# Gates multiplied in place in six broadcast buffers, and two kinds of store issued by ScalarE instead of SyncE

## The chip, the cores and the metric

The kernel runs on one core of a Trainium2 chip. The metric is the device time of one execution in microseconds (us), the median of several runs; lower is better. The profile is of one separate execution, in which every engine's instructions and the DMAs are recorded. Engines are named as in the profile: PE is TensorE, PEld its weight loads, DVE is VectorE, ACT is ScalarE, POOL is GpSimd, SP is SyncE. A "q" after the name (SPq) means the engine's sequencer, which issues DMAs and waits.

## The reference

Two layers on 32 images of 128 channels by 56 x 56 (3,136 tokens of 128 values each). What matters here is the second half of layer 1, a mixture of eight experts of which each token uses two:

```python
# layer 0
x = x + conv3x3(sign(groupnorm(x)), sign(w)) * Alpha
# layer 1
t = tokens(x)                                   # (32, 3136, 128)
n = layernorm(t)
t = t + (n @ Wq + bq) * sum_over_tokens((n @ Wk + bk) * (n @ Wv + bv))
n = layernorm(t)
p = softmax(n @ router_w + router_b)            # 8 experts
top_p, top_i = top_k(p, 2); top_p /= top_p.sum()
expert_out = einsum('bnd,edc->bnec', n, expert_w) + expert_b
t = t + einsum('bnk,bnkc->bnc', top_p, take(expert_out, top_i))
```

## The kernel before, in words

**Two ways to compute the experts.** A chunk is 128 tokens; an image has 25, the last of 64; a block is four chunks (512 tokens). The first blocks of each image (`DENSE`: 8 chunks of images 0 to 15, 12 of images 16 to 27, all 25 of images 28 to 31) are computed densely, with all eight experts and a gate that is zero for six of them. The other chunks are sorted by their pair of experts: their rows are scattered to DRAM (L1365), loaded again as tiles of one pair (L1662), multiplied by two experts (L1687), stored (L1730), gathered back by image (L1444), transposed (L1459), copied to a buffer `o` (L1467) and stored to the output (L1471).

**The dense path.** After routing, `gate_turn` transposes the gates into PSUM, `gate_out` (ACT, L1028 and L1033) copies them to `gt_sb` and, split in bf16 parts, to `gt_parts`. `gate_store` (SP, L1038) writes `gt_sb` to a DRAM tile `gp`, two of which alternate; `parts_store` (SP, L1061) writes the parts to `gb`. For block b and pair of experts k, a unit n, `spread` (SP, L1132) reads two rows of `gp` back, broadcast to all 128 partitions, into `bc`: 128 x 2 x 512 floats, 512 KB. With k = 0 it also loads the parts into `gt` (L1129, three DMAs). `gated` (DVE, L1141) multiplies the block's transposed tokens `tt` by both gate rows into a buffer `gated`; `experts` (PE, L1159) multiplies that by two expert matrices and accumulates over the eight experts in the PSUM bank `ff`; `finish` (DVE, L1170) adds the bank to `tt`, and `store` (SP, L1175) writes it out.

**Buffers.** `bc` has four buffers and `gated` two; `o` has two. A `bc` is free for the next `spread` when its `gated` step is done. A `gated` buffer is free when its matmuls are done.

**What sets the order.** No loop order is written. Each step is entered by `at` with a due time, an engine, a cost, the steps it comes after, the rings that it takes a buffer of and those that it frees. `in_order` (L116) plays the engines against these costs and fixes one order per engine for the whole kernel. Changing a ring's size, an engine or a cost can therefore move any instruction. On the chip each engine keeps its order and waits on semaphores. SP issues the loads of x (L315), the broadcasts, the tile loads, the pads (L1584) and all stores, in one queue. ACT issues DMAs only in the first 17 us (weights and the second and third image). The DMAs that SP and ACT issue share eight completion semaphores, taken in turn in the program's order, and a DMA waits until the one eight places before it has landed.

Of the kernel before, what the change touches and what calls it, by code (L numbers as in the profile page):

```python
# [44 lines left out]
F32 = mybir.dt.float32  # L45
# [4 lines left out]
ALU = mybir.AluOpType  # L50
# [4 lines left out]
C = 128  # L55
# [3 lines left out]
N_EXP = 8  # L59
# [6 lines left out]
WIDE = PER * C  # L66
# [29 lines left out]
LAG = 0.12  # L96
BANKS, EMPTIES = ("ps", "acc", "ff"), 7.0
ROOM = dict(
    ps=5, acc=1, ff=2, y=3, qs=3, tt=4, bc=4, gt=2, gated=2,
    t_in=3, turned=2, v=3, w=2, back=12, sent=4, o=2,  # L100
)

# [83 lines left out]
def conv_attn_moe_kernel(  # L186
# [19 lines left out]
    nc = tc.nc  # L206
    n_img, _, height, width = x.shape
# [29 lines left out]
    bpool = ctx.enter_context(tc.tile_pool(name="bpool", bufs=3))  # L237
    dpool = ctx.enter_context(tc.tile_pool(name="dpool", bufs=2, space=DRAM))
    ps = ctx.enter_context(tc.tile_pool(name="ps", bufs=5, space=PSUM))
# [45 lines left out]
    rb_bc = const.tile([C, N_EXP], F32, name="rb_bc")  # L285
    n_g = 9 * N_EXP
    eb9 = spool.tile([n_g, C], F32, tag="bq_kv", name="eb9")
    eb_row = bpool.tile([1, N_EXP * C], F32, tag="gated", bufs=2, name="eb_row")
    w_bin = const.tile([C, TAPS, C], BF16, name="w_bin")
    xs = const.tile([C, height + 2, width + 2], BF16, name="xs")  # L290
    nc.gpsimd.memset(xs, 0.0)
# [252 lines left out]
    def plan_image(i: int):  # L544
        s = base(i)
        d = {"x": x_all[i % HELD], "tok": tok_all[i % HELD]}
# [3 lines left out]
        n_sort = n_ck - n_dense  # L550
# [142 lines left out]
        for b in range(n_conv):  # L693
# [4 lines left out]
                take=["ps"],  # L698
# [5 lines left out]
        for g in range(n_blk):  # L704
            b = min(n_conv - 1, (cols_of(g)[1] - 1) // (ROWS * width))
            due = s + 4 + 5.5 * b
# [4 lines left out]
                take=["ps"],  # L711
# [105 lines left out]
        for g in range(n_blk):  # L817
# [8 lines left out]
                take=[] if g else ["acc"], free=[("y", ("scaled", i, g))],  # L826
# [208 lines left out]

        def gate_store():
            gp = dpool.tile([n_gb, N_EXP, WIDE], F32, tag="gp", name=f"gp_{i}")
            nc.sync.dma_start(  # L1038
                gp.rearrange("(h b) e (c t) -> (b e c) h t", h=max(1, n_half // 2), c=PER),
                d["gt_sb"],  # L1040
            )
            d["gp"] = gp
# [11 lines left out]
        def parts_store():  # L1054
# [37 lines left out]
            + [("gate_store", i - 1)],  # L1092
        )
        at(
            s + 138, ("gate_store", i), "SP", 0.45, gate_store,
            after=[("gate_out", i), ("spread", i - 2, last_units(i - 2))], delay=GATE_LANDS,
        )
        at(
# [24 lines left out]
        def spread(b, k):  # L1123
            n = cols_of(b)[1] - cols_of(b)[0]
            if k == 0:
                gt = bpool.tile([n_g, WIDE], BF16, tag="gt", bufs=2, name=f"gt_{i}_{b}")
                rows = d["gb"][b, :, :, :n].rearrange("j e t -> (j e) t")
                for r in range(0, n_g, n_g // 3):
                    nc.sync.dma_start(gt[r : r + n_g // 3, :n], rows)  # L1129
                d["gt", b] = gt  # L1130
            bc = bpool.tile([C, 2, WIDE], F32, tag="bc", bufs=4, name=f"bc_{i}_{b}_{k}")
            nc.sync.dma_start(  # L1132
                bc[:, :, :n],
                d["gp"][b, 2 * k : 2 * k + 2, :n].unsqueeze(0).to_broadcast([C, 2, n]),
            )
            d["bc", b, k] = bc

        def gated(b, k):
            n = cols_of(b)[1] - cols_of(b)[0]
            g = bpool.tile([C, 2, WIDE], F32, tag="gated", bufs=2, name=f"gated_{i}_{b}_{k}")  # L1140
            nc.vector.tensor_tensor(  # L1141
                g[:, :, :n],
                d["tt", b][:, :n].unsqueeze(1).to_broadcast([C, 2, n]),
                d.pop(("bc", b, k))[:, :, :n],
                ALU.mult,
            )
            d["gated", b, k] = g

        def experts(b, k):
            n = cols_of(b)[1] - cols_of(b)[0]  # L1150
            if k == 0:
                d["ff", b] = ps_ff.tile([C, WIDE], F32, tag="ff", name=f"ff_{i}_{b}")
                nc.tensor.matmul(  # L1153
                    d["ff", b][:, :n], lhsT=eb_w, rhs=d.pop(("gt", b))[:, :n], start=True, stop=False
                )
            g = d.pop(("gated", b, k))
            for j in range(2):
                e = 2 * k + j
                nc.tensor.matmul(  # L1159
                    d["ff", b][:, :n],  # L1160
                    lhsT=ew_d[:, e * C : (e + 1) * C],
                    rhs=g[:, j, :n],
                    start=False,
                    stop=(e == N_EXP - 1),
                )
# [15 lines left out]
        for b in dense_blocks:  # L1181
            share = (cols_of(b)[1] - cols_of(b)[0]) / WIDE
            n = b * pairs
            at(
                begin + n * unit - 4, ("tt_turn", i, b), "PE", 0.45 * share, to_channels, b,
                after=[("project_add", i, c // Q_GROUP) for c in blocks[b]]
                + [("gated", i, n - 2), ("gate_turn", i)]
                + [("tt_turn", i, b - 1) if b else ("tt_turn", i - 1, last_dense(i - 1))],
                take=["ps", "tt"],
            )  # L1190
            at(
                begin + n * unit - 3, ("tt_out", i, b), "ACT", 0.47 * share, to_channels_out, b,
                after=[("tt_turn", i, b)], free=[("ps", ("tt_turn", i, b))],
            )
            for k in range(pairs):
                n = b * pairs + k
                at(
                    begin + n * unit - 12, ("spread", i, n), "SP", 0.43 + 1.3 * (k == 0), spread, b, k,
                    after=[("gate_store", i), ("spread", i, n - 1), ("spread", i - 1, last_unit)]
                    + ([("parts_store", i)] if k == 0 else []),  # L1200
                    take=["bc"] if k else ["bc", "gt"], delay=SPREAD_LANDS,
                )
                at(
                    begin + n * unit, ("gated", i, n), "DVE", 1.14 * share, gated, b, k,
                    after=[("spread", i, n), ("tt_out", i, b)]
                    + [("gated", i, n - 1) if n else ("gated", i - 1, last_unit)],
                    take=["gated"], free=[("bc", ("spread", i, n))], slack=0.5,
                )
                at(
                    begin + n * unit + 2, ("experts", i, n), "PE",  # L1210
                    (1.74 + 0.22 * (k == 0)) * share, experts, b, k,
                    after=[("gated", i, n), ("experts", i, n - 1)],
                    take=[] if k else ["ff"],
                    free=[("gated", ("gated", i, n))] + ([] if k else [("gt", ("spread", i, n))]),
                )
            at(
                begin + n * unit + 4, ("finish", i, b), "DVE", 0.60 * share, finish, b,
                after=[("experts", i, n)],
                free=[("ff", ("experts", i, b * pairs))],
            )  # L1220
            at(
                begin + n * unit + 5, ("store", i, b), "SP", 0.43, store, b,
                after=[("finish", i, b)], free=[("tt", ("tt_turn", i, b))], delay=STORE_LANDS,
            )
# [243 lines left out]

        def back_store(b):
            lo, hi = cols_of(b)  # L1470
            nc.sync.dma_start(  # L1471
                out[i].rearrange("c h w -> c (h w)")[:, lo:hi], d.pop(("o", b))[:, : hi - lo]
            )

# [8 lines left out]
        for b in range(n_dense // PER, n_blk):  # L1483
            share = len(blocks[b]) / PER
            for c in blocks[b]:
                at(
                    due + each * k / n_sort, ("gather", i, c), "POOL", 1.5, gather, c,
                    after=[("result_rows", i)]
                    + [("gather", i, c - 1) if k else ("gather", i - 1, n_ck - 1)]
                    + [("tile_store", group, q) for q in range(quads_of(group))],  # L1490
                    take=["back"], delay=GATHER_LANDS,
                )
                k += 1
            at(
                due + each * k / n_sort + 5, ("back_turn", i, b), "PE", 0.45 * share, back_turn, b,
                after=[("gather", i, c) for c in blocks[b]], take=["ps"],
                free=[("back", ("gather", i, c)) for c in blocks[b]],
            )
            at(
                due + each * k / n_sort + 6, ("back_out", i, b), "ACT", 0.47 * share, back_out, b,  # L1500
                after=[("back_turn", i, b)], take=["o"], free=[("ps", ("back_turn", i, b))],
            )
            at(
                due + each * k / n_sort + 8, ("back_store", i, b), "SP", 0.43, back_store, b,
                after=[("back_out", i, b)], free=[("o", ("back_out", i, b))], delay=STORE_LANDS,
            )

# [370 lines left out]
```

## Time and profile before

| | |
|---|---|
| Median of 3 runs | 2172.5 us (2171.1 to 2178.69) |
| The profiled execution | 2270.18 us, of which the span from first to last instruction is 2268.4 us |
| Mean granted TensorE clock in it | 0.975 |
| Busy, of the span | PE 2103.4, DVE 1970.1, ACT 1531.2, POOL 1041.1 us |
| `gated`, L1141 | 384 times, 450.7 us in all |
| `experts`, L1159 | 1536 matmul records, 711.5 us in all |
| DMA engines | 54.7% of their time for queue q1, 8.2% for q0, 0.8% for q10 |
| Moved | 448.58 MB, mean 198 GB/s |

The profiled execution is longer than the median of the runs, so sums from the profile are held against its own span. In a row of a group, the figures are the busy time in all, the mean of one in ns, the engine's idle time just before these instructions, and what ended most of it. In the rows of slices, the span is cut into 40 parts of 56.7 us and each digit is the busy share in tenths. In a row of waits, the engine and line that waited come first, then what ended the wait, then total us, times, and the longest. In a timeline, the columns are start, duration, engine, line, operation, and in brackets the idle time before it. A wait for several semaphores is put down to the one that came last.

### The profile page before, as it was taken

The numbers are of one execution on the slowest core, as the hardware profiler recorded it, in microseconds if no ns is written. First come the engines' busy times: TensorE is split into PE (matmuls) and PEld (weight loads), VectorE is DVE, ScalarE is ACT, GpSimd is POOL, SyncE is SP. The second block draws the span as 40 slices with busy tenths as digits, with TensorE's granted clock in tenths as the row PEclk, the third lists the DMA queues.
The fourth block names the chain that finished last, engine by engine and source line by source line (L and its number), as shares of the span: only waits on it lengthen the run. The fifth ranks groups of instructions, "written<-read, shape, count | busy, mean of one in ns | idle before, by whom it ended". The sixth has DMA issues, their size and how long they took to land.

```text
span 2268.4 us, 45320 instructions
## 1 busy us (share of the span) xinstructions
PE 2103.4 (93%) x12074; PEld 1449.1 (64%) x12074; DVE 1970.1 (87%) x6074; ACT 1531.2 (68%) x4917; POOL 1041.1 (46%) x1013
## 2 busy tenths in 40 slices
PE   5899999899999999789999999988999999999888
PEld 2666656557777776457676776655676666676544
DVE  4899999999989999688888889988898798789865
ACT  5667776668888887468777867655877776574311
POOL 3044443333433325466443644676654446233563
PEclk9989999999999999899999999999999999999999
DMA  4155544465665565377667766667767777878788
GB/s 166 30 175 177 167 153 141 138 184 184 203 186 165 176 181 168 110 219 252 194 202 220 226 198 202 215 214 240 225 195 232 217 203 247 249 214 270 222 278 273
DMA packets 324364, 448.58 MB, mean 198 GB/s; under 512 B 61832, under 2 KB 222128, under 8 KB 324112
## 3 DMA queue, kind: packets, MB, share of 16 engines
q1 hardware_dynamic: 294384, 382.80, 54.7%
q0 software_dynamic: 28144, 56.14, 8.2%
q10 hardware_dynamic: 1584, 6.75, 0.8%
q8 instruction: 102, 1.67, 0.3%
q14 instruction: 150, 1.23, 0.2%
HBM read 319.51 MB, written 126.00 MB: 196 GB/s over the span
## 4 chain that ended last, share of the span: by engine, by line
PE 42%; DVE 5%; DMA 3%; issue 2%; ACT 2%; another core or an unknown queue 1%; SPq 0%; POOL 0%; DVEq 0%; ACTq 0%; POOLq 0%
PE ff L1159 14%; PE to L1687 7%; PE cv L642 6%; PE q L863 3%; PE gram L744 3%; PE turn L1669 2%; PE back_ps L1459 2%; PE xt L667 2%; DVE gated L1141 1%; DMA back<-res,res_no 1%; PE l L1114 1%; DMA out_dram<-o 1%; PE ff L1153 1%; DMA bc<-gp 0%
## 5 line engine op out<-in xcount | busy, mean ns | idle before, releaser
L1365 POOL DMA_INDIRECT rows<-tok,row_no x428 | 524.3, 1225 | 570.5 <-ACT tok L1358 235.8
L1159 PE MATMUL ff<-gated,ew_d 128*128 128x512 f32 (+1 forms) x1536 | 711.5, 592 | 23.8 <-DVE gated L1141 19.8
L1444 POOL DMA_INDIRECT back<-res,res_no x428 | 485.4, 1134 | 464.1 <-PE back_ps L1459 264.1
L1141 DVE TENSOR_TENSOR gated<-tt,bc 128x1024 f32<-128x1024 f32 x384 | 450.7, 1180 | 92.2 <-PE ff L1159 29.9
L642 PE MATMUL cv<-xs,w_bin 128*128 128x440 bf16 (+3 forms) x2016 | 429.8, 362 | 18.5 <-ACT xs L599 10.0
L1159 PEld LDWEIGHTS ff<-gated,ew_d 128*128 128x128 f32 x1536 | 274.5, 193 | 258.6 <-issue 202.2
L1705 ACT ACTIVATE v<-to,t_in 128x128 f32<-128x128 f32 x528 | 255.3, 484 | 138.1 <-PE to L1687 74.6
L642 PEld LDWEIGHTS <-w_bin 128*128 128x128 bf16 x2016 | 200.1, 100 | 187.8 <-issue 38.3
L1687 PEld LDWEIGHTS to<-ew_s,turned 128*128 128x128 f32 x2112 | 260.8, 194 | 57.8 <-issue 32.4
L877 ACT ACTIVATE qs<-q,r 128x136 f32<-128x136 f32 (+1 forms) x800 | 247.6, 406 | 70.3 <-PE q L863 35.1
L1687 PE MATMUL to<-ew_s,turned 128*128 x2112 | 273.3, 279 | 18.2 <-ACT turned L1675 8.1
L735 ACT ACTIVATE y<-tok,r 128x128 f32<-128x128 f32 (+1 forms) x800 | 257.0, 428 | 24.3 <-PE gram L744 10.4
L863 PE MATMUL q<-move,x 128*128 128x144 f32 (+1 forms) x1600 | 239.9, 295 | 12.7 <-issue 3.7
L863 PEld LDWEIGHTS q<-move,x 128*128 128x128 f32 (+1 forms) x1600 | 213.6, 193 | 42.4 <-issue 21.1
L744 PEld LDWEIGHTS gram<-y 128*128 128x128 f32 (+1 forms) x1600 | 203.3, 192 | 53.9 <-issue 40.4
L744 PE MATMUL gram<-y 128*128 128x129 f32 (+1 forms) x1600 | 217.8, 281 | 12.9 <-issue 8.1
L682 DVE BATCH_NORM_STATS2 st<-tok 128x6 f32<-128x128 f32 (+1 forms) x800 | 185.4, 279 | 31.9 <-ACT tok L673 26.9
L1712 ACT ACTIVATE w<-to,t_in 128x128 f32<-128x128 f32 x528 | 208.6, 395 | 0.0
L893 DVE BATCH_NORM_STATS2 st<-tok 128x6 f32<-128x128 f32 (+1 forms) x800 | 198.1, 284 | 6.3
L673 ACT COPY tok<-xt 128x512 f32<-128x512 f32 (+1 forms) x224 | 121.2, 561 | 99.9 <-PE xt L667 71.6
L653 DVE SCALAR_TENSOR_TENSOR x<-cv,alpha_col,x 128x448 f32<-128x448 f32 x224 | 151.3, 676 | 40.1 <-PE cv L642 7.2
L890 DVE TENSOR_TENSOR tok<-tok,qs 128x408 f32<-128x408 f32 (+1 forms) x288 | 156.1, 542 | 29.4 <-ACT tok L882 24.1
(229 smaller groups left out, 2896.0 us busy)
## 6 DMA issues: line engine op xcount, KB each, us to landing
bc<-gp SPq DMA_DIRECT2D x368, 512.0 KB
x<-in_x_dram SPq DMA_DIRECT2D x116, 392.0 KB
t_in<-rows SPq DMA_DIRECT2D x528, 66.0 KB
res<-v SPq DMA_DIRECT2D x132, 256.0 KB
out_dram<-o SPq DMA_DIRECT2D x100, 256.0 KB
out_dram<-tt SPq DMA_DIRECT2D x92, 256.0 KB
rows<-zeros SPq DMA_DIRECT2D x116, 66.0 KB
rows<-tok,row_no POOLq DMA_INDIRECT x428
```

Source lines behind the costliest of these rows:

```text
L642: nc.tensor.matmul(cv[:, r0:r1, c0:c1], lhsT=w_bin[:, t, :], rhs=xs[:, b * ROWS + dy + r0 : b * ROWS + dy + r1, dx + c0 : dx + c1], start= ...
L735: nc.scalar.mul(y[:n, j, :C], d["tok"][:n, c, :C], d["r1"][:n, c : c + 1])
L744: nc.tensor.matmul(d["gram"], lhsT=y[:n, j, :C], rhs=y[:n, j, :], start=(c == 0), stop=(c == n_ck - 1),)
L863: nc.tensor.matmul(p[:n, k, :], lhsT=d["x"][:, c * C : c * C + n], rhs=move, start=True, stop=True,)
L877: nc.scalar.mul(qs[:n, k, :], p[:n, k, : C + N_EXP], d["r1"][:n, c : c + 1])
L1141: nc.vector.tensor_tensor(g[:, :, :n], d["tt", b][:, :n].unsqueeze(1).to_broadcast([C, 2, n]), d.pop(("bc", b, k))[:, :, :n], ALU.mult,)
L1159: nc.tensor.matmul(d["ff", b][:, :n], lhsT=ew_d[:, e * C : (e + 1) * C], rhs=g[:, j, :n], start=False, stop=(e == N_EXP - 1),)
L1365: dma = nc.gpsimd.indirect_dma_start(out=groups[group]["rows"], out_offset=bass.IndirectOffsetOnAxis(ap=d["row_no"][:n, c - n_dense : c - ...
L1444: dma = nc.gpsimd.indirect_dma_start(out=d["back", c][:n, :], out_offset=None, in_=groups[group]["res"][: quads_of(group) * WIDE, :], in_o ...
L1687: nc.tensor.matmul(p[:, k, j, :], lhsT=t[:, n * C : (n + 1) * C], rhs=ew_s[:, bass.ds(d["cols", q][j][n], C)], start=True, stop=True,)
L1705: nc.scalar.activation(d["v", q][:, n, :], p[:, k, 0, :], AF.Identity, bias=row[:, C + 2 : C + 3], scale=row[:, C : C + 1],)
L1712: nc.scalar.mul(d["w", q][:, n, :], p[:, k, 1, :], row[:, C + 1 : C + 2])
```

## The change

The product is written over the broadcast gates: `gated` writes into its `bc` tile, the two `gated` buffers are dropped, and `bc` has six buffers of the same size instead of four. Such a tile is now held from the broadcast until the matmuls have read it. `gate_store` and `back_store` are issued by ACT instead of SP, with planned costs of 0.40 instead of 0.45 and 0.43, and `gate_store` is due half a microsecond earlier. The start's bias row takes a `bc` buffer. Nothing that is computed changes. The line numbers of the new kernel are lower by four after L1141 and by none before it.

```diff
-    ps=5, acc=1, ff=2, y=3, qs=3, tt=4, bc=4, gt=2, gated=2,
+    ps=5, acc=1, ff=2, y=3, qs=3, tt=4, bc=6, gt=2,
...
-    eb_row = bpool.tile([1, N_EXP * C], F32, tag="gated", bufs=2, name="eb_row")
+    eb_row = bpool.tile([1, N_EXP * C], F32, tag="bc", bufs=6, name="eb_row")
...
         def gate_store():
-            nc.sync.dma_start(
+            nc.scalar.dma_start(
...
-            s + 138, ("gate_store", i), "SP", 0.45, gate_store,
+            s + 137.5, ("gate_store", i), "ACT", 0.40, gate_store,
...
-            bc = bpool.tile([C, 2, WIDE], F32, tag="bc", bufs=4, name=f"bc_{i}_{b}_{k}")
+            bc = bpool.tile([C, 2, WIDE], F32, tag="bc", bufs=6, name=f"bc_{i}_{b}_{k}")
...
         def gated(b, k):
-            g = bpool.tile([C, 2, WIDE], F32, tag="gated", bufs=2, name=f"gated_{i}_{b}_{k}")
+            g = d["bc", b, k][:, :, :n]
             nc.vector.tensor_tensor(
-                g[:, :, :n],
-                d["tt", b][:, :n].unsqueeze(1).to_broadcast([C, 2, n]),
-                d.pop(("bc", b, k))[:, :, :n],
-                ALU.mult,
-            )
-            d["gated", b, k] = g
+                g, d["tt", b][:, :n].unsqueeze(1).to_broadcast([C, 2, n]), g, ALU.mult
+            )
...
-            g = d.pop(("gated", b, k))
+            g = d.pop(("bc", b, k))
...
                     begin + n * unit, ("gated", i, n), "DVE", 1.14 * share, gated, b, k,
-                    take=["gated"], free=[("bc", ("spread", i, n))], slack=0.5,
+                    slack=0.5,
...
                     begin + n * unit + 2, ("experts", i, n), "PE",
-                    free=[("gated", ("gated", i, n))] + ([] if k else [("gt", ("spread", i, n))]),
+                    free=[("bc", ("spread", i, n))] + ([] if k else [("gt", ("spread", i, n))]),
...
         def back_store(b):
-            nc.sync.dma_start(
+            nc.scalar.dma_start(
...
-                due + each * k / n_sort + 8, ("back_store", i, b), "SP", 0.43, back_store, b,
+                due + each * k / n_sort + 8, ("back_store", i, b), "ACT", 0.40, back_store, b,
```

## The prediction

> **What bounds the kernel now.** I read the page from the top: the busy shares, the row of slices, the costliest groups, then the waits of VectorE, of TensorE and of SP's queue, and last the timeline of the final image.
>
> ```profile
> PE 2103.4 (93%) x12074; PEld 1449.1 (64%) x12074; DVE 1970.1 (87%) x6074; ACT 1531.2 (68%) x4917; POOL 1041.1 (46%) x1013
> ...
> PE   5899999899999999789999999988999999999888
> ...
> DVE  4899999999989999688888889988898798789865
> ACT  5667776668888887468777867655877776574311
> ...
> L1159 PE MATMUL ff<-gated,ew_d 128*128 128x512 f32 (+1 forms) x1536 | 711.5, 592 | 23.8 <-DVE gated L1141 19.8
> ...
> L1141 DVE TENSOR_TENSOR gated<-tt,bc 128x1024 f32<-128x1024 f32 x384 | 450.7, 1180 | 92.2 <-PE ff L1159 29.9
> ```
>
> TensorE is the bound: 93% busy, so 2268.4 - 2103.4 = 165 us idle, of which the table of 60 us stretches puts 26.5 us into the start (0 to 60, before the first convolution), which this change doesn't touch. The idle time that a schedule could win back is thus about 138 us, spread thin: 18.1 us lie in 2100 to 2220, and 13.2 us in 900 to 960, where the granted clock falls to 0.83, which no edit here changes. VectorE is a close second until 480 us, and in the tail it alternates with TensorE: each waits for the other.
>
> ```profile
> DVE gated L1141 <- PE ff L1159: 29.9, 30, 2.8
> ...
> DVE gated L1141 <- DMA bc<-gp: 21.7, 11, 5.2
> DVE gated L1141 <- remote: 17.0, 2, 15.8
> ...
> PE ff L1159 <- DVE gated L1141: 19.8, 20, 2.6
> ...
> SPq L1038 <- ACT gt_parts L1033: 204.9, 18, 32.9
> ...
> SPq L1132 <- DVE gated L1141: 109.4, 79, 4.5
> ...
> SPq L1471 <- ACT o L1467: 44.0, 24, 8.4
> ```
>
> Columns: total us, times, longest. The first row is what the in-place product takes away (a free `gated` buffer); the second and third are late broadcasts; the last three are SP standing still at the head of its queue, two of them at the stores that move. What such a stand costs is seen in the last image:
>
> ```profile
> 2197.05 0.00 SPq L1132 DMA_DIRECT2D bc<-gp  x1
> ...
> 2201.47 0.58 ACT L1467 COPY o<-back_ps 128x512 f32<-128x512 f32 x1 [9.14 <-remote]
> ...
> 2202.08 0.36 SPq L1471 DMA_DIRECT2D out_dram<-o  x1
> ...
> 2202.48 1.47 SPq L1132 DMA_DIRECT2D bc<-gp  x3
> ...
> 2208.75 1.22 DVE L1141 TENSOR_TENSOR gated<-tt,bc 128x1024 f32<-128x1024 f32 x1 [5.18 <-DMA bc<-gp]
> ```
>
> SP issued one broadcast at 2197.05, then stood 5.0 us at the store of `o`; three broadcasts came out right behind it, VectorE waited 5.18 us for the first, and TensorE 2.6 us after that.
>
> **What the Trainium skill says.** (1) "DMA: Bandwidth & Descriptors", "Queues, rings and completion order": SP and ScalarE each own a row of rings on the same 16 DMA engines, and an engine takes turns between rows by packets. So a store from ScalarE needn't stand behind the queued broadcasts. The page shows queue q1 with 294,384 packets against 1,584 on q10: the second row is nearly empty now; no run yet shows the turn-taking. (2) The same page, "Issuing engines are not separate DMA queues": issuing elsewhere "will only save the time on the sequencer". The trace's 0.35 to 0.45 us per issue, and the standing above, are that time. (3) "VectorE: DVE Perf Modes", "The perf-mode tier table": fp32 tensor_tensor has the 1x mode alone, so the output's place has no faster mode to lose. The trace agrees: 1219 ns for 1024 columns out of place, 681 ns for 512 in place (L1170, L1717). The 538 ns between them are 1.05 ns a column, which leaves 143 ns fixed in both: in place costs nothing extra.
>
> **The change part by part**, against the profiled 2268.4 us of span (2270.2 with what lies around it). The runs' median, 2172.5, is 0.957 of that, and I scale by it at the end.
>
> *In place, six buffers.* No instruction goes: 384 products, 450.7 us, stay. The wait for TensorE (29.9 us, 30 times) goes; 19.6 us of it lies in the tail (2095 to 2268), where TensorE is idle in turn. In the built order the products that wait on a TensorE semaphore fall from 256 of 384 to 12. What is late next is the broadcast or TensorE itself, which isn't faster; so of 29.9 us I take 7 on the path (bounds 0 and 20).
>
> *The ring.* Before, broadcast n needs product n-4, and that needs the experts' matmuls n-6, for there are two `gated` buffers. After, it needs matmuls n-6 directly. The new rule asks for less: the 1.22 us of the product and VectorE's queue drop out. In the built order before, 187 of 384 broadcasts are the fourth issued and not yet multiplied, none the fifth; after, 174 are the fourth to the sixth. What it adds: SP now waits for TensorE instead of VectorE, with the tile loads (L1662), x loads and stores of `tt` behind it; I cost that at nothing, since what it waits for came before the old wait; if TensorE stalls, those behind stall with it. Against it stand the 21.7 us of late broadcasts, 11 times, and part of the 17.0 (15.8 of those lie in the stretch of low clock). I take 8 us (0 to 25).
>
> *Stores of gathered outputs.* SP loses 128 issues of 0.41 us (52.6 us), which lay beside other work, and its stands before them, 102.8 us in the timeline of its queue. 34 of those were over 0.8 us, 86.6 us in all; where the next SP instruction followed within 0.15 us, and so had been ready, they sum to 41 us. A late broadcast, gate row or load has 5 to 10 us of lead, so most of that was covered, but not the 5.0 us above, the 8.5 at 2135 and the 3.6 at 2246. Also `o`, two buffers, comes free earlier: the stores issued 182 us in total after their copies ended, median 0.62. I take 10 us (0 to 30).
>
> *Stores of gates.* The 205 us are no gain: behind the store stand the parts store (L1061), which needs the same gates 1 to 2 us later, and broadcasts that need the store. SP's stand moves to L1061. Only where the store was late after its copy (19.3 us in all, 12 of 32 images, 1.5 in the last) is there something: 2 us (0 to 8).
>
> *ScalarE's side.* It gets 160 issues. The same instruction took it 0.40 to 0.48 us at the start (L323 to L326), and it must let its own copy finish first, some 0.1 us of overlap lost: 160 x 0.5 = 80 us on 1531 us busy, against 737 us idle. The cover is that idle time; where it is thin (52.2 of 60 us busy in 1020 to 1080, 53.1 in 1680 to 1740, with five and four stores) the PSUM copies that free TensorE's banks come later. I take 4 us lost (0 to 40).
>
> *The added wait.* In the built order the hardware DMAs go round eight semaphores, and each waits for the one eight places before it. 141 of ScalarE's 160 stores so wait until a DMA of SP's has landed. Queued behind on ScalarE are `y`, `qs`, `tt`, `xt` and tile copies, and TensorE waits for those. In the times of before, that earlier DMA was issued after the copy ended for 13 of 128 stores, and within 4 us before it for 19 more; on the chain, broadcasts and stores landed after 1.9 to 6.8 us, so I put 9 us on the first and 2 us on the second. 13 x 9 + 19 x 2 = 155 us of ScalarE standing at worst, about half since SP now runs earlier. Most falls into ScalarE's idle time: 5 us on TensorE (0 to 75).
>
> Sum: 7 + 8 + 10 + 2 - 4 - 5 = 18 us of the profiled time, x 0.957 = 17. 2172.5 - 17 = 2155.
>
> **Rivals.** *The added wait decides (slower).* ScalarE stands at stores whose semaphore SP hasn't released, SP itself held by TensorE, and TensorE then finds no banks. For it: the in-order engine and 88% load of ScalarE in stretches. Against: TensorE's waits for ScalarE sum to 42 us now, the longest 3.4. With 155 us standing it cancels the gains when 15% reaches TensorE ((27 - 4) / 155), and from 22% it is slower by over 0.5%. At a third: 52 + 4 - 27 = 29, x 0.957 = 28: 2200; I centre this case on 2192. Chance 0.22.
>
> *TensorE takes it all (no difference).* The waits removed are VectorE's, and TensorE had 9s in most slices: what VectorE gains it loses at the next matmul, and the changed order shifts a few us either way. For it: 20 waits, 19.8 us, are all that TensorE spends at L1159 on products. Only the 5 us of the last image remain: 2168. Chance 0.22.
>
> *More than the sum.* The tail from 2095 leaves TensorE idle 25.2 us; if the second row of rings and the deeper ring win most of it, and the middle gives its upper bounds, 40 us: 2134. Chance 0.12.
>
> *In place is slower on VectorE*: excluded by L1170 and L1717.
>
> **How the numbers follow.** My forecast has 0.44 and runs from 2144 to 2161. Beyond 0.5% (11 us, about what a measurement of this kernel can tell from no change) on the fast side lie the forecast and the third rival, 0.56; within it 0.22; slower 0.22. The range runs from 2125, short of the far end of the third rival, to 2198, the last tenth of the slower case left out.
>
> **What would show it.** Right: no VectorE wait on L1159 at the products; the wait for broadcasts under 15 us; SP's longest stand at L1061; TensorE busy over 107 of the 120 us that end 50 us before the last (101.9 now). Wrong: "ACT out_dram" or ScalarE's copies waiting on landings for tens of us, TensorE waits on ScalarE above 50 us, or TensorE's idle time unchanged at 165.

## The result, and the profile after

The changed kernel takes 2204.0 us (median of 4 runs, 2200.6 to 2209.3) against 2175.6 us (4 runs, 2171.1 to 2182.6): ratio 1.0129, 95% interval 1.0107 to 1.0151. It is slower by 28 us; the forecast was 2155.

The profiled execution of before (2270.2 us) can't be set beside that of after (2209.3 us): the same kernel takes 2172 to 2177 us on some chips and 2261 to 2278 us on others, and only ratios taken on one chip are used below. A second profiled execution of before, the first of the experiments, took 2174.6 us (span 2172.9), and "before" means that one from here on.

The page of before, second execution, in its first line:

```profile
PE 2067.8 (95%) x12074; PEld 1437.0 (66%) x12074; DVE 1965.6 (90%) x6074; ACT 1529.0 (70%) x4917; POOL 1046.9 (48%) x1013
```

The page of after: busy shares, the row of slices for TensorE and VectorE, two DMA queues, and two groups.

```profile
PE 2072.6 (94%) x12074; PEld 1439.8 (65%) x12074; DVE 1968.0 (89%) x6074; ACT 1534.9 (70%) x4917; POOL 1069.9 (48%) x1013
...
PE   5899989898999999989999999999799998999887
...
DVE  4899999999999999989898999998788998879864
...
q1 hardware_dynamic: 271856, 353.82, 51.7%
...
q10 hardware_dynamic: 24112, 35.73, 4.5%
...
L1155 PE MATMUL ff<-bc,ew_d 128*128 128x512 f32 (+1 forms) x1536 | 711.2, 594 | 35.3 <-DVE bc L1141 35.0
...
L1141 DVE TENSOR_TENSOR bc<-tt,bc 128x1024 f32<-128x1024 f32 x384 | 446.9, 1178 | 65.9 <-DMA bc<-gp 58.0
```

The moved stores show on q10 (1,584 packets before, 24,112 now). The product in place costs VectorE nothing: 1178 ns a time, 1180 before. No engine has more instructions. TensorE, VectorE and ScalarE are busy for 2 to 6 us more, GpSimd for 23 us more (1046.9 to 1069.9, at 48% of the span, and its spans are rough). What grew most is the time in which TensorE stands: 2207.3 - 2072.6 = 135 us against 2172.9 - 2067.8 = 105 us. The waits say at what. Those of before, in the second execution (total us, times, longest):

```profile
DVE gated L1141 <- PE ff L1159: 48.9, 51, 4.6
...
DVE gated L1141 <- DMA bc<-gp: 18.6, 9, 4.9
...
PE ff L1159 <- DVE gated L1141: 16.2, 15, 3.2
...
PE back_ps L1459 <- DMA back<-res,res_no: 9.7, 9, 3.6
```

The same of after:

```profile
DVE bc L1141 <- DMA bc<-gp: 58.0, 41, 5.5
...
PE ff L1155 <- DVE bc L1141: 35.0, 25, 5.2
...
PE back_ps L1455 <- DMA back<-res,res_no: 22.3, 10, 5.2
...
DVE tt L1166 <- PE ff L1155: 20.6, 14, 2.9
```

The wait that the change was to remove, VectorE at the product for a free buffer (48.9 us), is gone. In its place VectorE waits for broadcasts (18.6 to 58.0), TensorE for products (16.2 to 35.0) and for gathered rows (9.7 to 22.3). SP's own queue in the kernel after:

```profile
SPq L1061 <- DVE gt_parts L1052: 269.2, 30, 26.7
...
SPq L1132 <- PE ff L1155: 119.6, 68, 5.3
...
SPq L1132 <- DMA out_dram<-o: 44.0, 15, 7.4
...
SPq L1129 <- DMA out_dram<-o: 16.1, 8, 7.8
```

The first two rows were foreseen: SP's stand moves to L1061, and broadcasts wait for matmuls. The last two were not. A broadcast and a load of gate rows wait for the landing of a gathered output's store, whose data they don't touch. All of SP's waits for such a landing sum to 71.6 us after and 6.8 us before.

A table computed from the records of TensorE's matmuls places the loss: how long TensorE had stood (us) by the time it had done so many us of work. The columns between the first and the last are experiments of the next section. Each column is one execution; a few us between columns mean nothing.

| TensorE's work done | before | old order, in place | ring alone, own plan | order of after, SP stores | after |
|---|---|---|---|---|---|
| 100 | 36.7 | 37.2 | 35.0 | 35.1 | 35.1 |
| 500 | 58.2 | 62.3 | 67.6 | 66.4 | 66.3 |
| 1300 | 70.8 | 75.5 | 81.4 | 81.5 | 82.6 |
| 1500 | 79.5 | 83.9 | 89.1 | 95.4 | 101.8 |
| 1900 | 84.7 | 89.4 | 96.6 | 101.9 | 109.2 |
| all | 102.0 | 105.1 | 108.7 | 117.1 | 131.6 |

After loses 9.7 us against before between 100 and 500, 10.5 us between 1300 and 1500, and 7.3 us from 1500 on. The first gathered output is stored at 892.7 us, long after the first of these stretches, so there these stores can't be the cause by being executed.

### The profile page after: what moved, and what is told of

Read it like the earlier page. It is cut to its first block, busy times and chain, and to the rows that moved or that the text cites. A ratio compares the mean times of both kernels' runs of the same rounds, so it can differ in the third digit from the quotient of the medians.

```text
span 2207.3 us, 44936 instructions
## 1 busy us (share of the span) xinstructions
PE 2072.6 (94%) x12074; PEld 1439.8 (65%) x12074; DVE 1968.0 (89%) x6074; ACT 1534.9 (70%) x4917; POOL 1069.9 (48%) x1013
## 3 DMA queue, kind: packets, MB, share of 16 engines
q10 hardware_dynamic: 24112, 35.73, 4.5%
## 4 chain that ended last, share of the span: by engine, by line
PE 59%; DVE 24%; DMA 9%; ACT 3%; issue 2%; SPq 1%; POOL 0%; DVEq 0%; ACTq 0%; POOLq 0%
PE ff L1155 20%; PE cv L642 11%; PE to L1683 9%; PE gram L744 5%; PE q L863 4%; DVE bc L1141 4%; DVE st L893 3%; DVE st L682 3%; DVE tok L890 2%; DMA bc<-gp 2%; PE xt L667 2%; PE turn L1665 2%; DVE tok L815 2%; DMA back<-res,res_no 2%; DVE x L653 2%
## 5 line engine op out<-in xcount | busy, mean ns | idle before, releaser
L1361 POOL DMA_INDIRECT rows<-tok,row_no x428 | 556.0, 1299 | 549.3 <-ACT tok L1354 242.7
L1155 PE MATMUL ff<-bc,ew_d 128*128 128x512 f32 (+1 forms) x1536 | 711.2, 594 | 35.3 <-DVE bc L1141 35.0
L1141 DVE TENSOR_TENSOR bc<-tt,bc 128x1024 f32<-128x1024 f32 x384 | 446.9, 1178 | 65.9 <-DMA bc<-gp 58.0
L1155 PEld LDWEIGHTS ff<-bc,ew_d 128*128 128x128 f32 x1536 | 278.2, 194 | 280.4 <-issue 211.7
L642 PE MATMUL cv<-xs,w_bin 128*128 128x440 bf16 (+3 forms) x2016 | 422.1, 358 | 13.5 <-ACT xs L599 12.9
L735 ACT ACTIVATE y<-tok,r 128x128 f32<-128x128 f32 (+1 forms) x800 | 252.3, 419 | 30.6 <-DVE r L527 18.8
L744 PEld LDWEIGHTS gram<-y 128*128 128x128 f32 (+1 forms) x1600 | 198.5, 191 | 35.6 <-issue 25.2
L744 PE MATMUL gram<-y 128*128 128x129 f32 (+1 forms) x1600 | 211.2, 278 | 3.1 <-ACT y L735 3.1
L682 DVE BATCH_NORM_STATS2 st<-tok 128x6 f32<-128x128 f32 (+1 forms) x800 | 184.4, 276 | 18.3 <-ACT tok L673 17.6
L1354 ACT ACTIVATE tok<-tok,a 128x128 f32<-128x128 f32 (+1 forms) x428 | 166.3, 434 | 5.5 <-ACT o L1463 2.6
```

Of the source, the lines that this page charges most:

```text
L642: nc.tensor.matmul(cv[:, r0:r1, c0:c1], lhsT=w_bin[:, t, :], rhs=xs[:, b * ROWS + dy + r0 : b * ROWS + dy + r1, dx + c0 : dx + c1], start= ...
L682: nc.vector.bn_stats(st[:n, c, :], d["tok"][:n, c, :C])
L735: nc.scalar.mul(y[:n, j, :C], d["tok"][:n, c, :C], d["r1"][:n, c : c + 1])
L744: nc.tensor.matmul(d["gram"], lhsT=y[:n, j, :C], rhs=y[:n, j, :], start=(c == 0), stop=(c == n_ck - 1),)
L1141: nc.vector.tensor_tensor(g, d["tt", b][:, :n].unsqueeze(1).to_broadcast([C, 2, n]), g, ALU.mult)
L1155: nc.tensor.matmul(d["ff", b][:, :n], lhsT=ew_d[:, e * C : (e + 1) * C], rhs=g[:, j, :n], start=False, stop=(e == N_EXP - 1),)
```

## The experiments

Three theories. *Landing*: SP's loads wait for stores that ScalarE issues late, because they share completion semaphores. *Ring*: SP stands for the experts' matmuls and holds its queue. *Order*: the planner, given new rings and engines, writes a worse order.

**Before again, and the parts.** The kernel before, unchanged:

> The kernel before, unchanged, for a second profiled execution: the first one (2270.2 us) is some 96 us longer than its own timed runs. Every theory expects 2171 to 2183 us, and an execution whose stretches can be set beside those of the kernel after (2209.3 us). The theories differ in what they then expect of the lines. Landing theory (a load on SP's queue waits for the landing of a store that ScalarE issued late, because they share a completion semaphore): before, SP waits for the landing of the gathered outputs' stores by under 20 us where after has 60.1 (44.0 + 16.1), and VectorE waits for the broadcasts by 20 to 30 us where after has 58.0. Order theory (the planner's new order is the worse one, whatever the engines): both of these are nearly equal, and the 28 us lie in PE's waits for VectorE and for the sorted rows.

It took 2174.6 us. Its rows are above: both 6.8 us of landings and 18.6 us of late broadcasts were nearer to what the landing theory expected.

Each part with the plan that it leads to:

```diff
# ring alone: all of the diff but the two dma_start lines and their two planned costs
# stores alone: those four lines only
```

> Gates multiplied in place in six buffers, planned so; both kinds of store stay with SP, in the plan too. Of the 28 us to be placed (2175.6 before, 2204.0 after): the ring theory (SP now waits for the experts' matmuls to give a buffer back, and holds the loads behind) puts most of them here, 2195 to 2205. The landing theory puts nothing here, 2165 to 2180, and some 7 us of gain may show. The order theory has the new order of this ring's rule in it: anything within 2165 to 2205, and decides only together with the kernel that keeps the old order.

> Both kinds of store issued and planned on ScalarE; four broadcast buffers and two for the product as before. Landing theory: the 28 us are here, 2195 to 2210, with SP waiting some 60 us for landings of the gathered outputs' stores (L1471 here). Ring theory: nothing of the loss here, 2160 to 2178. Order theory: undecided by this alone.

The ring alone: 2183.8 us, ratio 1.0032 (1.0021 to 1.0043). The stores alone: 2181.6 us, 1.0022 (1.0011 to 1.0033). Neither takes the 28 us, and both together would be 0.54% of the 1.29%: the rest comes only where both are planned at once.

**Order and execution taken apart.** The kernel after in all that it executes, with the planner told the old rings, engines and costs, so that TensorE, VectorE and GpSimd have before's instruction order (and SP and ScalarE too, but for the moved stores):

```diff
-    ps=5, acc=1, ff=2, y=3, qs=3, tt=4, bc=6, gt=2,
+    ps=5, acc=1, ff=2, y=3, qs=3, tt=4, bc=4, gt=2, gated=2,
-            s + 137.5, ("gate_store", i), "ACT", 0.40, gate_store,
+            s + 138, ("gate_store", i), "SP", 0.45, gate_store,
...
-                    slack=0.5,
+                    take=["gated"], free=[("bc", ("spread", i, n))], slack=0.5,
...
```

> The kernel after in all that it executes (in place, six buffers, both stores issued by ScalarE), but its planner is fed with the rings, engines and costs of the kernel before, so that the order of the work is that of before. Order theory: the loss goes away, 2160 to 2180. Landing theory and ring theory: the loss stays, 2195 to 2210, since neither the shared completion semaphores nor the buffers given back by the experts' matmuls depend on the plan.

2177.7 us, 1.0007 (0.9997 to 1.0017). Nearly the whole loss goes with the order. This excludes the ring theory as a cost of the execution itself, and leaves the landing theory with only a small part. Two more make a square of it: the order of after with SP issuing the stores, and the old order in place with SP issuing them.

> The counterpart of the kernel that kept the old order: the order of the work is that of the kernel after, six buffers, gates multiplied in place, but SP issues both kinds of store again, at the places where the new order has them. Order theory (28 us come with the planner's new order, whoever issues the stores): 2195 to 2212. Landing theory in a weaker form (the new order and ScalarE's stores together are needed for the loss): 2180 to 2190, that is the time of the ring alone.

> The order of the kernel before, gates multiplied in place in six buffers, both stores on SP. Order theory: no loss, 2168 to 2180, and this is the place where what the in-place product itself brings can be read, since nothing else differs from before; the prediction had put 7 us of gain there, 2169. Ring theory (SP standing for the experts' matmuls costs time of itself): 2180 to 2190, as the ring with its own plan gave 2183.8.

| ratio to before (95%) | SP issues both stores | ScalarE issues both |
|---|---|---|
| order of before, in place | 0.9985 (0.9977 to 0.9993) | 1.0007 (0.9997 to 1.0017) |
| order of after, in place | 1.0096 (1.0070 to 1.0122) | 1.0129 (1.0107 to 1.0151) |

The order of after with SP's stores took 2194.6 us, just below what the order theory expected (2195 to 2212) and above the weaker landing theory's 2180 to 2190. Each ratio is to before on the same chip; the four come from more than one chip. Down the columns the order costs 1.11% (1.0096 / 0.9985; the intervals together give 0.27% either way) and 1.22% (0.24%). Along the rows the issuing engine costs 0.22% (0.13%) and 0.33% (0.34%). The product in place brings 0.15%, 3 us: this version, 2172.3 us, is faster than both kernels. Read down the left column and then to the right, the 28 us are -3 (product in place), +24 (order) and +7 (issuing engine).

How little the removed wait was worth is seen in the old order with the product in place:

```profile
DVE bc L1141 <- DMA bc<-gp: 25.7, 15, 5.6
DVE tt L1166 <- PE ff L1155: 23.2, 20, 3.3
PE ff L1155 <- DVE bc L1141: 15.8, 18, 3.0
DVE bc L1141 <- ACT tt L1121: 13.8, 9, 6.4
```

Against the 48.9 us that went, VectorE waits 18.3 us more at the sum at L1166 (4.9 before), 13.4 more for the token copy (0.4 before) and 7.1 more for broadcasts; TensorE's wait for products is what it was (15.8, 16.2 before).

Then the kernel after without one of its two moves of stores:

> The kernel after with the store of gates left on SP, in the plan too: in place, six buffers, only the gathered outputs' stores moved to ScalarE. Alone the ring gave 2183.8 (+7) and both stores 2181.6 (+5); together they are +28, so some 16 us belong to neither alone. Order theory: those 16 us hang on where this one plan puts the sorted rows of the images 26 and 27 (11.5 us of TensorE's standing lie between the 1400th and 1500th us of its work), and any edit of the plan may remove them: 2180 to 2190 is likelier than 2200 to 2210. A theory in which the two moved stores act by what they execute expects 2195 to 2205 here, as the gathered outputs are 128 of the 160 moved stores.

> The kernel after with the gathered outputs' stores left on SP, in the plan too: in place, six buffers, only the store of gates moved to ScalarE. Order theory: anything from 2180 to 2205, by the luck of the plan; the sum of the ring alone and nothing else is 2184. A theory in which the stores act by what they execute expects 2183 to 2188, since only 32 of 160 stores are moved.

With only the gathered outputs' stores moved: 2196.2 us, 1.0091 (1.0068 to 1.0113). With only the stores of gates moved: 2191.0 us, 1.0087 (1.0066 to 1.0108). The first lies within what a theory of executed stores expected (2195 to 2205) and outside the likelier range of the order theory (2180 to 2190), the second above the 2183 to 2188 of the former. Neither removes the whole loss, and with 32 moved stores it is as large as with 128: their number doesn't set it, and what the planner makes of the move must have a part.

**What the order does.** TensorE's timeline around 322 us, in the kernel before (start, duration, in brackets the idle time before):

```profile
318.72 0.80 PE L863 MATMUL q<-move,x 128*128 128x144 f32 x4
322.35 3.37 PE L642 MATMUL cv<-xs,w_bin 128*128 128x448 bf16 x9 [2.83 <-ACT xs L599]
325.52 0.53 PE L1153 MATMUL ff<-gt,eb_w 72*128 72x512 bf16 x1
325.88 3.60 PE L1159 MATMUL ff<-gated,ew_d 128*128 128x512 f32 x8
```

The same place in the kernel after:

```profile
319.47 2.17 PE L863 MATMUL q<-move,x 128*128 128x144 f32 x14 [0.59 <-ACT tok L882]
321.57 0.39 PE L1149 MATMUL ff<-gt,eb_w 72*128 72x512 bf16 x1
327.18 2.08 PE L1155 MATMUL ff<-bc,ew_d 128*128 128x512 f32 x2 [5.21 <-DVE bc L1141]
```

Before, nine matmuls of a convolution stand ahead of the experts; TensorE waits 2.8 us for their input, and the product (VectorE, 323.5) is ready when they end. After, the experts come first and TensorE stands 5.2 us; the product starts at 325.9. The same gap is there at 425 us (5.2 us). Between 100 and 500 us of TensorE's work its waits for products rise from 1.1 to 15.4 us, and all others fall from 20.4 to 15.8: this is the 9.7 us of that stretch.

**Is any other plan worse, or this one?** Two kernels leave everything of before but one planner constant: the cost of a gathered output's store, 0.43 to 0.40 (TensorE's order stays 99.8% the same), and the landing time of a broadcast, 6.5 to 7.0 (91%).

> The kernel before with its own buffers and engines; only one number of the planner is changed, and by 0.03 us: the cost of a gathered output's store on SP, 0.43 to 0.40. Fitted-plan theory (the constants of the planner have been fitted until this one order came out well, so nearly any other order is worse): 2178 to 2190 if the few places that move matter. Rule theory (what costs 22 us is the ring's rule and the engine in the new plan, not that the plan is another): 2172 to 2178.

> The kernel before again, with one number of the planner changed by half a microsecond: the landing time of a broadcast, 6.5 to 7.0. As many instructions change places as between the kernels before and with both stores moved. Fitted-plan theory: 2180 to 2205. Rule theory: 2170 to 2179, as a later landing asks nothing that the hardware can't give.

With them ran two kernels on what the stores on ScalarE cost, both in the old order and in place: only the gathered outputs' stores on ScalarE, and SP's stores with extra work for ScalarE:

```diff
+            pad = bpool.tile([C, 128], F32, tag="pad", bufs=1, name=f"pad_{i}_{b}")
+            nc.scalar.copy(pad, ident)
+            nc.scalar.copy(pad, ident)
```

> The order of the kernel before, six buffers and the product in place; SP issues the store of gates as before, ScalarE issues the 128 stores of gathered outputs. The same order with both stores on SP took 2172.3, with both on ScalarE 2177.7. Landing theory (SP's broadcasts wait for the landing of gathered outputs that ScalarE issued late: 50 us of such waits with both moved, 2 to 7 with none): nearly all of the 5 us is here, 2175.5 to 2178, with 40 to 50 us of SP waiting for these landings. Gate theory (the longer way from the store of gates to the broadcasts): nothing here, 2171 to 2174.

> The same order, both stores on SP, and ScalarE executes two further copies of 128x128 (some 0.27 us each, nobody reads them) beside each store of gathered outputs: about 68 us of ScalarE's time against the 43 us that 128 stores of 0.34 us took there. Issue theory (what costs is ScalarE's time): 2177 to 2181. Landing theory (ScalarE has the time to spare, what costs is that SP waits for its stores): 2171 to 2174.5.

All four ran where before takes 2277.7 us and scatters more: 0.9982 (0.9961 to 1.0004) for the small nudge, 1.0029 (1.0003 to 1.0054) for the other, 1.0024 (1.0002 to 1.0046) for the gathered outputs' stores, 1.0019 (0.9996 to 1.0042) for the extra work. These intervals are too wide to tell the theories apart, but for the small nudge: less than 0.05% lost. The other three were taken again, with a fourth that tells the planner a much later landing:

```diff
-GATE_LANDS, SPREAD_LANDS, STORE_LANDS, TILE_LANDS, GATHER_LANDS = 5.0, 6.5, 5.0, 6.0, 12.0
+GATE_LANDS, SPREAD_LANDS, STORE_LANDS, TILE_LANDS, GATHER_LANDS = 5.0, 10.0, 5.0, 6.0, 12.0
```

> The kernel with the old order, the product in place, and only the gathered outputs' stores on ScalarE, once more, as its first comparison was too coarse (1.0024, interval 1.0002 to 1.0046). The same without the moved stores was 0.9985 of before, with both kinds moved 1.0007. Landing theory: 1.0000 to 1.0012. Gate theory: 0.9980 to 0.9990.

> The old order, the product in place, both stores on SP, and two copies of some 0.3 us (80 us of ScalarE's time in all) beside each of the 128 stores, once more (1.0019, interval 0.9996 to 1.0042 in the first comparison). Landing theory: 0.9980 to 0.9992, as without the copies. Issue theory: 1.0010 to 1.0040, twice the 0.0022 that both moved stores cost.

> The kernel before, whose planner is told that a broadcast lands after 7.0 us and not after 6.5, once more (1.0029, interval 1.0003 to 1.0054 in the first comparison). In its trace TensorE stood 5.7 us twice ahead of the experts (at 224 and 429 us), as in the kernel after (5.2 us, at 322 and 425). Fitted-plan theory: 1.0020 to 1.0100. Rule theory: 0.9985 to 1.0010.

> In place, six buffers, both stores on SP, its own plan (that was 1.0032), and the planner is told that a broadcast lands after 10.0 us and not after 6.5. In the new order the experts' matmuls stand ahead of the next image's convolution in the images 6, 8 and 10, up to 5 us before VectorE's product is there; told a later landing, the planner puts 18 of the convolution's matmuls ahead of the experts in all of the images 3 to 9. Order theory: TensorE's standing in its first 500 us of work falls from 67.6 us to 57 to 62, and the whole by as much, to 0.9980 to 1.0010, if the later images' order, which moves too, takes nothing back. Fitted-plan theory alone (another plan, another loss): 1.0000 to 1.0080.

The nudge of 0.5 us: 1.0019 (1.0006 to 1.0031). Another plan does cost something, but about a sixth of the 1.11% of after's order. The late landing, in place with its own plan: 1.0074 (1.0048 to 1.0100), a miss. TensorE's standing at 500 us fell by only 2 us (67.6 to 65.5), and the end grew. The 5 us gaps were gone, and six shorter ones (2.5 to 3.1 us) stood ahead of the convolution: here, a later landing cured one wait and didn't give a better plan.

The gathered outputs' stores on ScalarE: 1.0026 (1.0015 to 1.0037), against 0.9985 without. That is more than either theory expected. The extra work, 42.0 + 38.2 = 80 us on ScalarE: 1.0006 (0.9991 to 1.0020), between the ranges of the two theories. So ScalarE's time, at 43 us of issues, explains about a quarter of the 0.41% that these stores cost: 80 us cost 0.21% (0.17% either way), 43 us in proportion 0.11%, and 0.20% at the far end of that interval. The rest fits the landings, which sum in SP's queue to 50.9 us here and 7.7 us with the extra work. VectorE's wait for broadcasts, in the kernel with these stores on ScalarE:

```profile
DVE bc L1141 <- DMA bc<-gp: 38.9, 20, 6.1
```

and in the one with the extra work:

```profile
DVE bc L1141 <- DMA bc<-gp: 24.0, 17, 4.3
```

One such landing, in the tail of the former. From the timelines of SP, ScalarE's queue, ScalarE and VectorE, in order of time:

```profile
2117.13 1.22 SPq L1129 DMA_DIRECT2D gt<-gb  x3
2117.20 0.59 ACT L1463 COPY o<-back_ps 128x512 f32<-128x512 f32 x1 [7.19 <-PE back_ps L1455]
2117.82 0.34 ACTq L1467 DMA_DIRECT2D out_dram<-o  x1
...
2124.19 0.82 SPq L1132 DMA_DIRECT2D bc<-gp  x2
...
2129.18 1.23 DVE L1141 TENSOR_TENSOR bc<-tt,bc 128x1024 f32<-128x1024 f32 x1 [4.21 <-DMA bc<-gp]
```

SP issues nothing from 2118.4 to 2124.2; the trace puts 5.8 us of that down to the landing of a store of `o`. ScalarE could issue its store only after the copy, which had waited 7.2 us for TensorE. The broadcasts come out late, and VectorE waits 4.2 us for one of them. SP's stand at the store wasn't removed: it was put off by up to eight DMAs. That the landing itself is what costs was not tried apart from the engine that issues. One rival can be read from the traces: the broadcasts' packets aren't slower for the second queue beside them, since a packet of q1 takes 66.2 ns on average with these stores on ScalarE and 66.3 ns with them on SP, in the old order both times.

**Which rule of the planner.** The new ring changes two rules: a broadcast's buffer is held until the experts, and a product needn't wait any more until the experts two before it are done, since it takes no buffer of its own. Two kernels keep the second rule in the planner (nothing executes it), the first one with SP's stores, the second one with all else of after:

```diff
-    ps=5, acc=1, ff=2, y=3, qs=3, tt=4, bc=6, gt=2,
+    ps=5, acc=1, ff=2, y=3, qs=3, tt=4, bc=6, gt=2, gated=2,
...
-                    slack=0.5,
+                    take=["gated"], slack=0.5,
...
-                    free=[("bc", ("spread", i, n))] + ([] if k else [("gt", ("spread", i, n))]),
+                    free=[("bc", ("spread", i, n)), ("gated", ("gated", i, n))] + ([] if k else [("gt", ("spread", i, n))]),
```

> In place, six buffers taken by the broadcast and given back by the experts, both stores on SP, its own plan, with one rule of the kernel before kept in the planner: a product waits until the experts two before it are done, though it has no buffer of its own any more. Without that rule the plan gave 1.0032. With it 97.5% of TensorE's instructions stand as in the kernel before, against 78% without. Two-ahead theory (the loss comes from the planner letting products and experts run further ahead of each other, which moves the experts ahead of the convolution): 0.9975 to 1.0005, TensorE's standing at 500 us of its work 57 to 63 us. Buffer theory (the loss comes from the broadcasts, which are now given six buffers and held until the experts): 1.0020 to 1.0050, as that part of the rule is unchanged.

> The kernel after in all parts (in place, six buffers, both stores planned for and issued by ScalarE), with the same one rule kept in the planner. The kernel after is 1.0129. Two-ahead theory: what is left is the stores on ScalarE in a plan of their own (1.0022 with the buffers of before) less what the product in place brings (0.0015): 0.9995 to 1.0030. Fitted-plan theory (any plan that moves this much costs about as much as after's): 1.0060 to 1.0130.

In place with SP's stores: 0.9993 (0.9968 to 1.0017). After in all else: 1.0002 (0.9974 to 1.0030), which excludes the 1.0129 of after without the rule, with the reserve that these two ran where before takes 2261 us and after itself wasn't timed there. Three other kernels were timed on a slower and on a faster chip (2277.7 and 2171.5 us for before): 1.0029 and 1.0019, 1.0024 and 1.0026, 1.0019 and 1.0006, so a ratio carried over to about 0.1%. TensorE's timeline at the place shown above is that of before again, in the first of the two:

```profile
325.50 1.82 PE L642 MATMUL cv<-xs,w_bin 128*128 128x448 bf16 x9 [2.84 <-ACT xs L599]
327.15 0.38 PE L1149 MATMUL ff<-gt,eb_w 72*128 72x512 bf16 x1
327.96 2.41 PE L1155 MATMUL ff<-bc,ew_d 128*128 128x512 f32 x5 [0.43 <-DVE bc L1141]
```

How far each plan's order is from before's can be counted in the traces: the longest sequence of TensorE's instructions that stands in both, as a share of all, where an instruction is named by its line and its place among those of this line. (The expectations give other figures, 97.5% and 78% for the third and the eighth row, by another way of matching.)

| plan | order kept | ratio |
|---|---|---|
| before's own, in place | 100% | 0.9985 |
| before, cost 0.43 to 0.40 | 99.8% | 0.9982 |
| in place, rule kept | 97.0% | 0.9993 |
| after, rule kept | 92.5% | 1.0002 |
| before, landing 7.0 | 91.3% | 1.0019, 1.0029 |
| stores alone | 89.3% | 1.0022 |
| after without the gates' stores moved | 82.5% | 1.0091 |
| ring alone | 82.3% | 1.0032 |
| order of after, SP stores | 81.8% | 1.0096 |
| after | 81.8% | 1.0129 |
| after without the outputs' stores moved | 81.7% | 1.0087 |
| in place, landing 10.0 | 80.3% | 1.0074 |

Dropping the rule moves the most, and the plans that drop it cost the most. But the distance doesn't set the cost: the ring alone is as far from before as the other five of them and loses less than half of what they lose. Why one such order loses 0.3% and another 1% wasn't found. GpSimd's longer busy time isn't it: at least 1068 us in five of these six plans, and 1050.1 in the last, which loses 0.74%. Whether products that run freely ahead are bad in themselves, or bad only with due times and costs that suit the old rule, stays open.

## Why the prediction was wrong, step by step

**The ring is the step that failed.** The prediction took +8 us for it, since "the new rule asks for less", with a lower end of 0. On the chip that is so: with the old order, buffers and waits of the new rule lose nothing (0.9985). But fewer constraints in the planner don't make a better order. It read from the built order how many broadcasts are ahead, and never asked what else had changed places: 18% of TensorE's order. With its own plan the ring gave 1.0032 / 0.9985 = 0.47% lost, some 10 us, and with the stores' plan on top 1.1%, some 24 us. The front part of the document had the fact ("can therefore move any instruction"); no term of the sum, and no rival, had the order in it beyond "a few us either way".

**The sizes came from a slower execution.** The waits were read from the profiled 2268.4 us and scaled by 0.957. In the second execution of before TensorE's busy time is less by 2% (2067.8 against 2103.4 us), its standing by 36% (105 against 165 us), and VectorE's wait for a `gated` buffer is longer (48.9 against 29.9 us). So one factor doesn't carry waits from one execution to the other; of the 138 us that a schedule could win back, some 78 are there at the speed of the timed runs (105.1 less 26.7 at the start).

**In place**: right in kind, with the size near the low end. +7 us (0 to 20) forecast, 3 us measured (0.15%, 0.07 to 0.23). The stall went, and what was late next was TensorE, at the sum instead of at the product; TensorE's own wait didn't shrink.

**Stores of gathered outputs**: +10 us (0 to 30) forecast, together with the gates' +2, ScalarE's -4 and the wait's -5 a gain of 3. Measured in the old order: a loss of 0.22%, 5 us, for both kinds, and of 0.41%, 9 us, for the gathered outputs alone. That the second is more than the first would mean that the gates' stores gain on ScalarE; that wasn't tried alone in the old order, and the two ratios come from different chips. The gain counted SP's stand at the store as removed, and point (2) of what the prediction takes from the Trainium skill adds this stand to the sequencer's time. The sentence that it quotes ("DMA: Bandwidth & Descriptors", "Issuing engines are not separate DMA queues") speaks only of the time to initiate a DMA, here 0.34 us on ScalarE. The stand comes back at most eight DMAs later, as a wait for the landing.

**The added wait** was seen from one side only. The prediction counted the 141 stores of ScalarE that wait for one of SP's DMAs, 155 us at worst; in the trace of after ScalarE stands for such a landing once, 1.4 us. In the same built order 134 DMAs of SP carry a wait for a store of ScalarE's, 39 of them broadcasts and 28 loads of gate rows, and the runs speak for a cost on that side: 71.6 us of such waits, where TensorE's waits for ScalarE stayed at 23.1 us (19.9 before).

**Stores of gates, ScalarE's side**: SP's stand moved to L1061 (269.2 us), as forecast. A store's issue took ScalarE 0.34 us (gathered) and 0.42 us (gates), less than the 0.5 that was taken.

**The rival of the slower side** had the sign, and a time near the result (2192 to 2200), for another reason. ScalarE doesn't starve TensorE: TensorE's waits for ScalarE sum to 23 us after, far under the 50 that were to show it. *TensorE takes it all* describes the in-place part well, and nothing else.

Of the signs, two held: no wait of VectorE for the experts at the product, and SP's largest sum at L1061. Two said wrong: broadcasts waited for 58.0 us (under 15 expected), and TensorE was busy 52.2 + 52.7 = 105 of the 120 us from 2040 to 2160 (over 107 expected; before has 106.4 in its second execution, so the 101.9 of the first was no base for this sign). Of the signs of being wrong the two of ScalarE didn't come; TensorE's idle time was to stay at 165 and grew, from 105 to 135 us.

## What to carry to other kernels

Where a planner orders the work, a buffer ring is also a rule of the planner: when the ring goes, decide whether the rule should go with it, and compare the two orders instruction by instruction before costing anything else. How many instructions moved says that there is something to cost, not how much. Test a change once with the old order frozen; that splits in one run what it does on the engines from what the replanning does. Before a DMA moves to another queue, look at both directions of what couples the queues: who now waits for it, and for whose DMAs it waits.

## What the runs showed of the hardware

The same kernel took 2172 to 2177 us on three of the chips and 2261 to 2278 us on two others, 4 to 5%, with the same busy time on VectorE (1965.6 and 1970.1 us) and the same bytes moved. Of the two executions of before, the longer one has a mean granted TensorE clock of 0.975 (0.984 in the other), and 0.83 between 900 and 960 us (0.98); TensorE is busy 36 us longer in it and stands 60 us longer. What causes this was not tested. The issue of a gathered output's store cost ScalarE 0.34 us, a little less than SP (0.39 to 0.41 on average in the two executions of before). The fp32 product of 128x1024 took VectorE 1178 ns in place and 1180 ns out of place.
